# Two attention stages in a woven Trainium2 kernel: first attention by query only and turned by TensorE, second attention's scores copied and masked by a GpSimd select

## The chip, the cores and the metric

The program runs on one core of one Trainium2 chip (the chip has eight). The metric is device time in microseconds of one execution: 2770.05 us for the kernel before, the median of three runs (2768.12 to 2773.97). A core has five engines that work beside each other, each through its own instructions in order: TensorE (PE, with its weight loads shown apart as PEld), VectorE (DVE), ScalarE (ACT), GpSimd (POOL) and SyncE (SP), which here starts the DMAs. [...]

## The reference, cut to what matters

Two layers over x, 16 batches of 256 tokens by 256 channels, float32 throughout:

```python
x = x + _L0_attn_ref(_L0_cond_ref(x, f, f, ...), ...)      # cross attention, then the first attention
x = x + _L0_ffn_ref(_L0_cond2_ref(x, ...), ...)            # a category's matrix, then a quantized feed-forward
x = x + _L1_attn_ref(_L1_cond_ref(x, ...), ...)            # diffusion, then the second attention
x = x + _L1_ffn_ref(_L1_cond2_ref(x, ...), ...)            # an expert's projection, then a mixture of experts
```

The change touches the two causal attentions. The first has 16 heads of width 16 over the 256 tokens:

```python
scores = jnp.einsum('bhtd,bhsd->bhts', q, k) / jnp.sqrt(jnp.float32(Dh))
scores = jnp.where(causal, scores, -jnp.inf)
probs = jax.nn.softmax(scores, axis=-1)
out = jnp.einsum('bhts,bhsd->bhtd', probs, v)
```

The second has 16 heads of width 64 over segments of 128 tokens, with 16 learned keys and values ahead of each segment's own:

```python
mask = (j < p) | (j - p <= i)
scores = jnp.where(mask, scores, NEG_INF)
attn = jax.nn.softmax(scores, axis=-1)
out = jnp.einsum('bhij,bhjd->bhid', attn, v)
```

## The kernel before, in words

`program` runs `woven` (everything up to the second attention, for all batches) and then `mixture` (the last feed-forward, line 1266 and on). The change touches `woven` alone.

`woven` has a stage for each step of a batch, written as a Python generator that yields one instruction at a time: stage_a (cross attention and the first attention's projection), stage_m and stage_e (first attention), stage_gate, stage_up and stage_down (quantizing the feed-forward's weights, once), stage_y and stage_f (category matrix and feed-forward), stage_d (diffusion), stage_p and stage_u (second attention's projections of q, k and of v), stage_g (its scores), stage_v (its values and output), stage_c (an early start of the mixture) and stage_fill. `weave` (line 188) merges them while the program is built: it keeps a clock for each engine, takes at each step the instruction that could start first by the cost model in `Unit.cost` (line 167), ties by the stage's place in the list, and issues it. So the order of each engine's queue is fixed at build time, by planned durations. All instructions of the woven part carry line 163, where they are issued, and groups are told apart by the names of their tiles.

Stages wait for each other through counters in `g.done`: J counts batches projected, M and E halves through stage_m and stage_e, A batches whose first attention is done, D batches diffused, P, U, G and V the items of the second attention (four a batch, 64 in all). Stage_a projects batch b when `M >= 2 * b and A >= b - 1` (line 413). PSUM is handed out as two pairs (two banks each) and four singles; `quad` takes both pairs. Stage_fill keeps TensorE busy with matmuls of the identity (tile `ident` alone) in planned gaps until the first batch's first attention is done.

The first attention treats the heads of a batch in two halves of eight. The 128 channels of a half lie on the partitions: four groups of 32, two heads in each. `blocks` spreads a transposed q or k by head (b_diag) so that a group's matmul of 32 rows gives the scores of its two heads; the four groups' matmuls go to different rows of TensorE. A half passes twice through its scores:

- `heads_maximum` (stage_m): transposes q and k (b_qk to b_qkT), scores with the queries on the partitions, adds the mask and takes the maximum on VectorE, and exponentials on ScalarE, of which only the sums are kept. Maxima and reciprocal sums (tile `shift`) are transposed into `b_rows`.
- `heads_exponential` (stage_e): the scores again, now with the keys on the partitions (b_diag, b_qkT), and by matmuls of `ones` with b_sdiag the negated maxima on top in PSUM. One exponential for each pair (b_e), and a GpSimd select that zeroes the keys behind the query.
- `heads_values`: the values' matmuls on b_e (32 columns of weights), the reciprocal sums spread over the channels by a matmul (`spread`), two VectorE steps to b_u and a GpSimd sum to b_oT. Stage_e then applies the output projection (wout, b_oT).

The second attention's `scores4` (stage_g) makes the scores of four heads for two segments (keys, f_q), adds the mask on VectorE while copying from PSUM to f_prob, and then takes maxima (f_stat), exponentials and sums, and GpSimd's product with the reciprocal sums. `values4` (stage_v) transposes f_prob on TensorE (f_prob to f_pT), multiplies with the values (f_pT, f_v to f_oT) and applies the output projection (wo, f_oT). `project4` (stage_p) makes q and k: VectorE products, GpSimd sums (f_t), and eight DMAs for an item that move the rows into f_q and keys.

Of the kernel before, what the change touches and what calls it, by code (L numbers as in the profile page):

```python
# [19 lines left out]
P = 128  # L20
# [128 lines left out]
class Unit:  # L149
# [17 lines left out]
    def cost(self, fn, outs, ins):  # L167
        if self.name == "SP":
            return 0.5
        if self.name == "PE":  # L170
            if fn == "transpose":
                return 0.13
            lhsT, rhs = ins
            rows, cols, t = lhsT.shape[0], row_size(lhsT), row_size(rhs) / 555

            if rows <= 64:
                return SIDE
            return max(t / 3.5, 0.1) if cols <= 32 else max(t / 1.7, 0.14) if cols <= 64 else t
        fixed, each = COSTS[self.name]
        n = max(row_size(x) for x in outs[:1] + ins)  # L180
        if fn == "reciprocal":
            each = 0.006
        if fn == "affine_select":
            fixed, each = 0.2, 0.00095
        return fixed + each * n + (0.3 if len(outs) > 1 else 0)
# [108 lines left out]
S_BUFS = 2  # L294
# [19 lines left out]
def woven(k):  # L314
    nc, tc = k.nc, k.tc
    with ExitStack() as ctx:
        g = Stages()
        g.k, g.a, g.B, g.ident = k, k.a, k.B, k.ident
        g.pe, g.dve, g.act = Unit("PE", nc.tensor), Unit("DVE", nc.vector), Unit("ACT", nc.scalar)
        g.pool, g.sp = Unit("POOL", nc.gpsimd), Unit("SP", nc.sync)  # L320
        pool = lambda name, bufs, **kw: ctx.enter_context(tc.tile_pool(name=name, bufs=bufs, **kw))
        g.w = pool("w", 1)
        g.xp = pool("x", 5)
        g.f_, g.l_ = pool("sf", 1), pool("sl", 1)

        g.attention0 = tc.tile_pool(name="sa", bufs=1, side="right")
        g.a_ = g.attention0.__enter__()
        space = bass.MemoryType.PSUM
        psum = pool("psum", 1, space=space)
        g.pairs = [psum.tile([P, 2, 512], F32, name=f"pair{i}") for i in range(PAIRS)]  # L330
        g.singles = [psum.tile([P, 512], F32, name=f"single{i}") for i in range(8 - 2 * PAIRS)]
        g.zT = {}
        g.v1, g.live, g.kT, g.qk, g.v = {}, {}, {}, {}, {}
        g.taking = False
        g.x, g.io, g.done = {}, {}, {"J": 0, "U": 0, "Y": 0, "H": 0, "W": 0, "D": 0, "Z": 0, "A": 0, "M": 0, "E": 0, "F": 0, "P": 0, "G": 0, "V": 0, "L": 0, "R": 0, "C": 0}
        with tc.manual_schedule():
            weave([stage_a(g), stage_m(g), stage_e(g), stage_gate(g), stage_up(g), stage_down(g), stage_y(g), stage_f(g), stage_v(g), stage_g(g), stage_p(g), stage_u(g), stage_d(g), stage_c(g), stage_fill(g)])
# [80 lines left out]
def head_constants(g):  # L418
# [9 lines left out]
    g.halves, g.place = small("halves", 2), small("place", 32)  # L428
    yield g.dve.tensor_reduce(g.halves, g.ident.rearrange("p (g r d) -> p r g d", g=4, r=2), AX.XY, ALU.add)
    yield g.dve.tensor_reduce(g.place, g.ident.rearrange("p (g w) -> p w g", g=4), AX.X, ALU.add)  # L430
    g.ones, g.spread = small("ones", P), small("spread", P)
    yield g.pool.memset(g.ones, 1.0)
    own = g.ident.rearrange("p (g w) -> p g w", g=4)[:, :, 2:4]
    yield g.pool.tensor_copy(g.spread.rearrange("p (g r d) -> p g r d", g=4, r=2), own.unsqueeze(3).to_broadcast([P, 4, 2, DH0]))
    g.shift = small("shift", 2, P)
    yield g.pool.memset(g.shift, 0.0)


def stage_m(g):

    for i in range(2 * g.B):
        yield lambda: g.done["J"] > i // 2 and i < g.done["E"] + 2
        g.kT[i] = yield from heads_maximum(g, i)
# [3 lines left out]
def stage_e(g):  # L447

    for b in range(g.B):
        oT = g.a_.tile([P, 2, S], F32, name="b_oT", tag="b_oT")  # L450
        for c in range(2):
            yield lambda: g.done["M"] > 2 * b + c
            kept = g.kT.pop(2 * b + c)
            prob = yield from heads_exponential(g, *kept)
            yield from heads_values(g, b, c, prob, kept[1], oT)
# [166 lines left out]
def blocks(g, name, src, which, bufs):  # L622


    t = g.a_.tile([P, 2, S], F32, name=name, tag=name, bufs=bufs)
    wide = [P, 2, S]
    yield g.pool.tensor_tensor(t, src.unsqueeze(1).to_broadcast(wide), which.unsqueeze(2).to_broadcast(wide), ALU.mult)
    return t


def heads_maximum(g, i):
# [4 lines left out]
    t = g.a_.tile([P, 2, S], F32, name="b_qkT", tag="b_qkT", bufs=2)  # L636
# [8 lines left out]
    kd = yield from blocks(g, "b_diag", t[:, 1, :], g.halves, 2)  # L645
    shift = g.shift
    by_head = shift.rearrange("p s (g w) -> p s g w", w=32)
    sums = g.a_.tile([P, 2, 4, 2], F32, name="b_sums", tag="b_sums", bufs=2)
    for st in (1, 0):
# [6 lines left out]
        scores = []  # L656
        for two in four:
            sc = g.a_.tile([P, 2, 2, n], F32, name="b_s", tag="b_s", bufs=S_BUFS)
            raw = two[:, :, : 2 * n].rearrange("p i (r k) -> p i r k", r=2)
            mask = g.k.mask[:, 2 * P - n :].unsqueeze(1).unsqueeze(1).to_broadcast([P, 2, 2, n])  # L660
            yield g.dve.tensor_tensor(sc, raw, mask, ALU.add)
            g.pairs.append(two)
            scores.append(sc)
        for j0, sc in zip((0, 2), scores):
            yield g.dve.tensor_reduce(by_head[:, st, j0 : j0 + 2, 0:2], sc, AX.X, ALU.max, negate=True)
        for j0, sc in zip((0, 2), scores):
            for j in (j0, j0 + 1):
                for r in range(2):
                    x, one = sc[:, j - j0, r, :], lambda t, w: t[:, st, j, w : w + 1]
                    yield g.act.activation(x, x, AF.Exp, bias=one(by_head, r), accum_out=one(sums, r))  # L670
    yield g.dve.reciprocal(by_head[:, :, :, 2:4], sums)
    rows = g.a_.tile([P, S], F32, name="b_rows", tag="b_rows", bufs=2)
    one = yield from single(g, shift)
    pt = one[:, :S]
    for st in range(2):
        yield g.pe.transpose(pt[:, st * P : (st + 1) * P], shift[:, st, :], g.ident)
    yield copy_(g, rows, pt)
    g.singles.append(one)
    return t, rows


def heads_exponential(g, t, rows):


    qd = yield from blocks(g, "b_diag", t[:, 0, :], g.halves, 2)
    sd = yield from blocks(g, "b_sdiag", rows, g.place[:, 0:2], 1)
    prob = []
    for kb in range(2):
        n = (2 - kb) * P
        four = yield from quad(g, t, qd, sd)  # L690
        out = lambda j: four[j // 2][:, j % 2, : 2 * n]
        for j in range(4):
            lhsT, rhs = t[row32(j, 32), 1, kb * P : (kb + 1) * P], qd[row32(j, 32), :, kb * P :]
            yield g.pe.matmul(out(j), lhsT, rhs, start=True, stop=False)
        for j in range(4):
            yield g.pe.matmul(out(j), g.ones[row32(j, 32), :], sd[row32(j, 32), :, kb * P :], start=False, stop=True)
        for two in four:
            e = g.a_.tile([P, 4, n], F32, name=f"b_e{kb}", tag=f"b_e{kb}", bufs=2)
            yield g.act.activation(e.rearrange("p (i r) k -> p i (r k)", i=2), two[:, :, : 2 * n], AF.Exp)
            g.pairs.append(two)  # L700
            own = e[:, :, 0:P]
            yield g.pool.affine_select(
                out=own,
                in_=own,
                compare_op=ALU.is_ge,
                fill=0.0,
                base=0,
                pattern=[[0, 4], [1, P]],
                channel_multiplier=-1,
            )  # L710
            prob.append(e)
# [3 lines left out]
def heads_values(g, b, c, prob, rows, oT):  # L715


    v = g.v[b]
    po = yield from single(g, *prob, v)
    by_half = po.rearrange("p (r s) -> p r s", r=2)  # L720
    for kb in range(2):
        for j in range(4):
            lhsT = v[:, kb, c * P + 32 * j : c * P + 32 * (j + 1)]
            e = prob[2 * kb + j // 2][:, 2 * (j % 2) : 2 * (j % 2) + 2, :]
            yield g.pe.matmul(by_half[row32(j, 32), :, kb * P :], lhsT, e, start=kb == 0, stop=kb == 1)
    one = yield from single(g, rows)
    yield g.pe.matmul(one[:, :S], g.spread, rows, start=True, stop=True)
    rinv = rows
    yield copy_(g, rinv, one[:, :S])
    g.singles.append(one)  # L730
    u = g.a_.tile([P, 2, S], F32, name="b_u", tag="b_sdiag")
    for r in range(2):
        yield g.dve.scalar_tensor_tensor(u[:, r, :], by_half[:, r, :], g.halves[:, r : r + 1], rinv, ALU.mult, ALU.mult)
    g.singles.append(po)
    yield g.pool.tensor_tensor(twined(oT[:, c : c + 1, :]), untwined(u[:, 0:1, :]), untwined(u[:, 1:2, :]), ALU.add)
# [446 lines left out]
def scores4(g, n, q, keys):  # L1182
# [10 lines left out]
    mask = g.k.mask[:, P - PM :].unsqueeze(1).unsqueeze(1).to_broadcast([P, 2, 2, w])  # L1193
    by_head = lambda t: t.rearrange("p (a j) w -> p j a w", a=2)
    for st in range(2):
# [8 lines left out]
        yield g.dve.tensor_tensor(by_head(prob[:, st]), raw, mask, ALU.add)  # L1204
        g.pairs.append(two)
    for st in range(2):
# [547 lines left out]
```

## Time and profile before

| what | value |
|---|---|
| median of three runs | 2770.05 us (2768.12 to 2773.97) |
| profiled execution | 2773.39 us, span 2771.7 us |
| granted TensorE clock, mean | 0.978 of full speed |
| TensorE busy | 2594.5 us (94% of the span) |
| VectorE, ScalarE, GpSimd busy | 1430.1, 1083.4 and 980.5 us (52%, 39%, 35%) |
| first and last output projection of the first attention | start at 121.8 and about 1566 us |
| last matmul of the woven part | ends about 1809 us |

The span's busy shares mix two programs: the woven part, in which four engines share the work, and the mixture behind it, in which TensorE is busy for 952 of 961 us. Stretches and groups of the woven part alone tell more than the page's first line. In a line of a group stand: line, engine, operation, tile written and tiles read, shape (rows by columns of weights, then partitions by elements), count; then the busy time in us and the mean of one in ns; then the engine's idle time just before the group and what ended it. A float32 matmul shows as two records, a transpose as one.

### The profile page before, as it was taken

What the parts mean: (1) busy time and instruction counts of PE and PEld (TensorE: products, weight loads), DVE (VectorE), ACT (ScalarE), POOL (GpSimd) and SP (SyncE); (2) the same over time, 40 slices, a digit from 0 to 9 for tenths busy, and PEclk for the clock granted to TensorE, in tenths of its full rate; (3) what the DMA queues carried; (4) which work ended last, traced back from release to release, by engine and by line L of the source; (5) the groups of instructions that cost most, each with busy time, mean ns of one, the idle gap of its engine ahead of it and who ended that gap; (6) DMA issues with size and microseconds to landing.
All of it is one profiled execution on the core that took longest, in us unless ns stands there. A gap on an engine that the chain in (4) does not pass through costs nothing. (4 is left out here: it accounts for less than half of the span.)

```text
span 2771.7 us, 40010 instructions
## 1 busy us (share of the span) xinstructions
PE 2594.5 (94%) x13855; PEld 1893.2 (68%) x13855; DVE 1430.1 (52%) x2712; ACT 1083.4 (39%) x3304; POOL 980.5 (35%) x1121
## 2 busy tenths in 40 slices
PE   8879898998999999999999898899999999999999
PEld 6645576666766666676665676555566888888866
DVE  7466676776777776777777665333340000000023
ACT  2444435444545544644554433322222222222221
POOL 5344545444445445454555433223320000000035
PEclk9999999999999999999999999899999999999999
DMA  4121333233343333233332254141111455556523
GB/s 127 51 77 37 97 116 97 87 103 101 94 126 106 96 96 122 62 114 118 104 95 86 73 157 125 58 131 51 50 45 69 150 190 197 186 194 199 200 84 107
DMA packets 249661, 303.64 MB, mean 110 GB/s; under 512 B 43120, under 2 KB 216432, under 8 KB 240112
## 3 DMA queue, kind: packets, MB, share of 16 engines
q1 hardware_dynamic: 243312, 284.26, 32.8%
q0 software_dynamic: 6144, 16.79, 1.9%
q8 instruction: 112, 1.84, 0.3%
q14 instruction: 93, 0.76, 0.1%
HBM read 206.85 MB, written 60.56 MB: 96 GB/s over the span
## 5 line engine op out<-in xcount | busy, mean ns | idle before, releaser
L1398 POOL DMA_INDIRECT got<-osort,pos_o x64 | 62.3, 974 | 626.4 <-ACT hT L1331 586.0
L1380 ACT ACTIVATE ehT<-bank,own_b 128x256 f32<-128x256 f32 x280 | 132.5, 473 | 349.1 <-PE bank L49 349.1
L163 POOL TENSOR_TENSOR f_t<-f_t,f_t 128x256 f32<-128x256 f32 x256 | 187.5, 750 | 210.2 <-DVE f_t L163 189.2
L163 PE MATMUL single<-e_zT,wq 128*128 128x256 f32 x1024 | 250.8, 388 | 0.0
L49 PE MATMUL bank<-ysT,w 128*128 128x256 f32 x1120 | 247.6, 379 | 0.2 <-ACT ysT L105 0.2
L49 PE MATMUL bank<-w,ehT 128*128 128x256 f32 x1120 | 247.5, 379 | 0.0
L163 ACT ACTIVATE b_s<-b_s,shift 128x128 f32<-128x128 f32 (+1 forms) x512 | 225.3, 444 | 55.4 <-DVE shift L163 55.4
L49 PEld LDWEIGHTS bank<-ysT,w 128*128 128x128 f32 x1120 | 212.7, 190 | 29.3 <-ACT ysT L105 0.5
L163 ACT ACTIVATE f_prob<-f_prob,f_stat 128x144 f32<-128x144 f32 x512 | 205.5, 405 | 60.3 <-DVE f_stat L163 60.2
L49 PEld LDWEIGHTS bank<-w,ehT 128*128 128x128 f32 x1120 | 210.2, 190 | 27.2
L163 PEld LDWEIGHTS single<-e_zT,wq 128*128 128x128 f32 x1024 | 190.0, 193 | 38.7 <-issue 11.0
L163 ACT ACTIVATE b_e<-pair 128x512 f32<-128x512 f32 (+1 forms) x128 | 99.9, 804 | 118.6 <-PE pair L163 118.1
L163 PE MATMUL single<-wo,f_oT 128*128 128x256 f32 x512 | 134.4, 397 | 12.0 <-DVE f_oT L163 9.9
L163 PE MATMUL pair<-b_diag,b_qkT 32*128 32x512 f32 (+1 forms) x1024 | 133.4, 545 | 12.5 <-POOL b_diag L163 5.9
L1388 DVE TENSOR_TENSOR eo<-bank,eb 128x512 f32<-128x512 f32 x35 | 24.2, 691 | 234.4 <-PE bank L49 234.4
L163 DVE TENSOR_TENSOR x<-x,single 128x512 f32<-128x512 f32 (+1 forms) x112 | 68.1, 608 | 132.9 <-PE single L163 129.9
L163 DVE TENSOR_TENSOR b_s<-pair,mask 128x512 f32<-128x512 f32 (+1 forms) x128 | 116.3, 949 | 19.6 <-PE pair L163 19.1
L163 PE MATMUL single<-wv,e_zT 128*128 128x256 f32 x512 | 122.2, 382 | 1.6 <-DVE x L163 1.6
L163 POOL TENSOR_TENSOR f_prob<-f_prob,f_stat 128x1024 f32<-128x1024 f32 x64 | 123.1, 1924 | 0.0
L1347 DVE COPY own_b<-b1t 128x8 f32<-128x8 f32 x35 | 5.9, 174 | 222.3 <-ACT ehT L1380 222.3
L1493 POOL DMA_INDIRECT ysort<-r_y,r_posi x64 | 62.4, 975 | 164.0 <-DMA ysort<-r_y,r_posi 105.4
L163 PEld LDWEIGHTS single<-wo,f_oT 128*128 128x128 f32 x512 | 97.0, 196 | 32.7 <-DVE f_oT L163 10.9
(313 smaller groups left out, 5366.2 us busy)
## 6 DMA issues: line engine op xcount, KB each, us to landing
w<-in_w SPq DMA_DIRECT2D x70, 1024.0 KB, 5.3
wq<-in_w_qk SPq DMA_DIRECT2D x128, 256.0 KB, 3.2
ysort<-zero SPq DMA_DIRECT2D x32, 1024.0 KB, 6.6
wv<-in_w_v SPq DMA_DIRECT2D x64, 256.0 KB, 3.7
f_q<-f_t SPq DMA_DIRECT2D x256, 64.0 KB, 2.0
keys<-f_t SPq DMA_DIRECT2D x256, 64.0 KB, 2.0
wo<-in_w_out SPq DMA_DIRECT2D x64, 256.0 KB, 3.5
ys<-ysort SPq DMA_DIRECT2D x35, 256.0 KB, 2.7
```

The lines of the kernel that those rows point to most:

```text
L49: nc.tensor.matmul(out, lhsT, rhs, start=start and i == 0, stop=stop and i == last)
L163: return Op([(self.name, self.cost(fn, outs, aps), lambda: call(*args, **kw))], outs, aps)
L1347: nc.vector.tensor_copy(b1, r.b1t[:, t, :])
L1380: nc.scalar.activation(hT[:, f, :], ph, AF.Gelu_apprx_tanh, bias=b1[:, f : f + 1])
L1388: nc.vector.tensor_tensor(o, po, b2.unsqueeze(1).to_broadcast([P, 2, D]), ALU.add)
L1398: nc.gpsimd.indirect_dma_start(out=g, out_offset=None, in_=k.osort[:, :], in_offset=bass.IndirectOffsetOnAxis(ap=r.pos_o[:, i, t : t + 1], ...
L1493: nc.gpsimd.indirect_dma_start(out=k.ysort[:, :], out_offset=bass.IndirectOffsetOnAxis(ap=posi[:, i, t : t + 1], axis=0), in_=ys[t], in_of ...
```

## The change

The first attention passes through its scores once. `heads_maximum` and `heads_exponential` become `heads_softmax`: with the queries on the partitions, it masks only the blocks on the diagonal on VectorE, copies the left block of the second 128 queries by ScalarE or VectorE, takes the maxima, the exponentials with their sums in place, the reciprocals, and GpSimd's product. `heads_values` then transposes the probabilities on TensorE (b_e), 24 blocks of 128x128 a half, copies them to b_pT, and runs the same values' matmuls on these; the two heads of a group are put together by two scaled steps instead of the spread matmul, b_u and the GpSimd sum. The tiles ones, spread, place and shift go. Stage_m now waits until the first two of the four head groups of the half before have been turned (counter T).

The second attention's `scores4` copies the scores by ScalarE or VectorE (`copy_` leaves the choice to `weave`) and masks them by a GpSimd select on the 128 own keys. Three costs in the planner's model are changed (a transpose 0.13 to 0.115, columns per us 555 to 580, the factor for narrow weights 1.7 to 1.5), and stage_v moves behind stage_d in the list of stages.

```diff
             if fn == "transpose":
-                return 0.13
+                return 0.115
             lhsT, rhs = ins
-            rows, cols, t = lhsT.shape[0], row_size(lhsT), row_size(rhs) / 555
...
                 return SIDE
-            return max(t / 3.5, 0.1) if cols <= 32 else max(t / 1.7, 0.14) if cols <= 64 else t
+            return max(t / 3.5, 0.1) if cols <= 32 else max(t / 1.5, 0.14) if cols <= 64 else t
...
-            weave([stage_a(g), stage_m(g), stage_e(g), stage_gate(g), stage_up(g), stage_down(g), stage_y(g), stage_f(g), stage_v(g), stage_g(g), stage_p(g), stage_u(g), stage_d(g), stage_c(g), stage_fill(g)])
+            weave([stage_a(g), stage_m(g), stage_e(g), stage_gate(g), stage_up(g), stage_down(g), stage_y(g), stage_f(g), stage_g(g), stage_p(g), stage_u(g), stage_d(g), stage_v(g), stage_c(g), stage_fill(g)])
...
 def stage_m(g):
 
     for i in range(2 * g.B):
-        yield lambda: g.done["J"] > i // 2 and i < g.done["E"] + 2
-        g.kT[i] = yield from heads_maximum(g, i)
+        yield lambda: g.done["J"] > i // 2 and g.done["T"] >= 2 * i - 1
+        g.kT[i] = yield from heads_softmax(g, i)
         g.done["M"] = i + 1
 
 
@@ -450,9 +442,7 @@
         oT = g.a_.tile([P, 2, S], F32, name="b_oT", tag="b_oT")
         for c in range(2):
             yield lambda: g.done["M"] > 2 * b + c
-            kept = g.kT.pop(2 * b + c)
-            prob = yield from heads_exponential(g, *kept)
-            yield from heads_values(g, b, c, prob, kept[1], oT)
+            yield from heads_values(g, b, c, g.kT.pop(2 * b + c), oT)
             g.done["E"] += 1
...
+    kd = g.a_.tile([P, 2, S], F32, name="b_diag", tag="b_diag")
+    wide = [P, 2, S]
+    yield g.pool.tensor_tensor(
+        kd, t[:, 1, :].unsqueeze(1).to_broadcast(wide), g.halves.unsqueeze(2).to_broadcast(wide), ALU.mult
+    )
+    prob = {}
+    mask = g.k.mask[:, P:].unsqueeze(1).unsqueeze(1).to_broadcast([P, 2, 2, P])
     for st in (1, 0):
         n = (st + 1) * P
...
+        stat = g.a_.tile([P, 3, 8], F32, name="b_stat", tag="b_stat", bufs=4)
+        for jp, two in enumerate(four):
+            e = prob[st, jp] = g.a_.tile([P, 4, n], F32, name=f"b_e{st}", tag=f"b_e{st}", bufs=3)
+            raw = two[:, :, : 2 * n].rearrange("p j (r k) -> p j r k", r=2)
+            sc = e.rearrange("p (j r) k -> p j r k", r=2)
+            yield g.dve.tensor_tensor(sc[:, :, :, n - P :], raw[:, :, :, n - P :], mask, ALU.add)
+            if st:
+                yield copy_(g, sc[:, :, :, :P], raw[:, :, :, :P])
             g.pairs.append(two)
+        for jp in range(2):
+            e, own = prob[st, jp], slice(4 * jp, 4 * jp + 4)
+            yield g.dve.tensor_reduce(stat[:, 0, own], e, AX.X, ALU.max, negate=True)
+            for h in range(4):
+                one = lambda w: stat[:, w, 4 * jp + h : 4 * jp + h + 1]
+                yield g.act.activation(e[:, h, :], e[:, h, :], AF.Exp, bias=one(0), accum_out=one(1))
+            yield g.dve.reciprocal(stat[:, 2, own], stat[:, 1, own])
+            yield g.pool.tensor_tensor(e, e, stat[:, 2, own].unsqueeze(2).to_broadcast([P, 4, n]), ALU.mult)
     return prob
...
+def heads_values(g, b, c, prob, oT):
+
+
+    v, turned = g.v[b], []
+    for jp in range(2):
+        t = g.a_.tile([P, 4, 3, P], F32, name="b_pT", tag="b_pT", bufs=2)
+        e = prob[0, jp]
+        one = yield from single(g, e)
+        pt = one.rearrange("p (h q) -> p h q", h=4)
+        for h in range(4):
+            yield g.pe.transpose(pt[:, h, :], e[:, h, :], g.ident)
+        yield copy_(g, t[:, :, 0, :], pt)
+        g.singles.append(one)
+        e = prob[1, jp]
+        for h0 in (0, 2):
+            one = yield from single(g, e)
+            pt = one.rearrange("p (h k q) -> p h k q", h=2, k=2)
+            for h in range(2):
+                for kb in range(2):
+                    yield g.pe.transpose(pt[:, h, kb, :], e[:, h0 + h, kb * P : (kb + 1) * P], g.ident)
+            yield copy_(g, t[:, h0 : h0 + 2, 1:, :], pt)
+            g.singles.append(one)
+        g.done["T"] += 1
+        turned.append(t.rearrange("p h k q -> p h (k q)"))
+    po = yield from single(g, *turned, v)
...
+            pT = turned[j // 2][:, 2 * (j % 2) : 2 * (j % 2) + 2, :]
+            rhs = pT[:, :, S:] if kb else pT[:, :, :S]
+            yield g.pe.matmul(by_half[row32(j, 32), :, kb * P :], lhsT, rhs, start=kb == 0, stop=kb == 1)
+    which, own = lambda r: g.halves[:, r : r + 1], twined(oT[:, c : c + 1, :])
+    first, other = untwined(by_half[:, 0:1, :]), untwined(by_half[:, 1:2, :])
+    a = g.act.activation(own, first, AF.Copy, scale=which(0))
+    d = g.dve.tensor_scalar(own, first, which(0), None, ALU.mult)
+    yield Op(a.choices + d.choices, a.outs, a.ins)
+    yield g.dve.scalar_tensor_tensor(own, other, which(1), own, ALU.mult, ALU.add)
     g.singles.append(po)
...
-    mask = g.k.mask[:, P - PM :].unsqueeze(1).unsqueeze(1).to_broadcast([P, 2, 2, w])
...
-        yield g.dve.tensor_tensor(by_head(prob[:, st]), raw, mask, ALU.add)
+        yield copy_(g, by_head(prob[:, st]), raw)
         g.pairs.append(two)
+        own = prob[:, st, :, PM:]
+        yield g.pool.affine_select(
+            out=own, in_=own, compare_op=ALU.is_ge, fill=NEG, base=0, pattern=[[0, 4], [-1, P]], channel_multiplier=1
+        )
```

## The prediction

> **What bounds the kernel now.** I read the page first, then the busy time in stretches, then who waited for whom on TensorE, then the groups of TensorE by shape. The profiled execution took 2773.4 us (span 2771.7 us; the median of the runs is 2770.05 us, so 3.3 us lie between it and the figure I forecast). The woven part, which the change touches, ends near 1810 us.
>
> ```profile
> 122.00:1640.00 1518.00, 1389.21 (x8285) 973.07 (x8285) 1093.53 (x1850) 723.80 (x2492) 729.17 (x833) 0.97 0.32 96
> 1640.00:1782.00 142.00, 120.94 (x731) 96.18 (x731) 71.48 (x117) 48.82 (x193) 49.56 (x60) 0.90 0.44 133
> ```
>
> Columns: stretch, length, then busy time of PE, PEld, DVE, ACT, POOL, the granted clock, DMA. From 122 to 1640 us TensorE is busy for 92%, VectorE for 72%, ScalarE and GpSimd for 48% each. So TensorE's own work is the bound, plus 129 us in which it waits:
>
> ```profile
> PE single L163 <- POOL d_h L163: 35.2, 13, 8.4
> PE single L163 <- DVE shift L163: 16.7, 10, 4.8
> PE pair L163 <- ACT b_e L163: 10.0, 12, 1.2
> ...
> PE single L163 <- POOL f_prob L163: 6.9, 6, 1.7
> ```
>
> Totals in us, times, longest. The second and third lines belong to steps that the change removes; the first and last stay.
>
> ```profile
> L163 PE MATMUL single<-ident,f_prob 128*128 128x128 f32 x512 | 82.1, 293 | 25.0 <-POOL f_prob L163 25.0
> L163 PE MATMUL pair<-b_diag,b_qkT 32*128 32x512 f32 x512 | 79.5, 657 | 7.5 <-POOL b_diag L163 5.9 <-DVE b_v L163 0.8 <-ACT a_e L163 0.8
> L163 PE MATMUL single<-ident 128*128 128x128 f32 x468 | 62.1, 288 | 1.6 <-POOL ident masks.py:199 1.6
> L163 PE MATMUL pair<-b_diag,b_qkT 32*128 32x256 f32 x512 | 53.9, 434 | 5.0 <-DVE b_s L163 2.8 <-ACT b_e L163 2.2
> L163 PE MATMUL pair<-b_sdiag,ones 32*128 32x512 f32 x256 | 38.4, 639 | 1.1 <-POOL b_sdiag L163 0.8
> L163 PE MATMUL pair<-b_sdiag,ones 32*128 32x256 f32 x256 | 25.2, 394 | 0.0
> L163 PE MATMUL single<-b_rows,spread 128*128 128x256 f32 x64 | 22.4, 431 | 1.7 <-DVE d_th L163 1.7
> L163 PE MATMUL single<-ident,shift 128*128 128x128 f32 x64 | 14.2, 306 | 19.1 <-DVE shift L163 16.7 <-DVE f_stat L163 1.5 <-ACT d_hT L163 0.9
> ```
>
> A transpose is one record, any other matmul two. The mean (293 ns) is a record's latency; what it costs in a stream is the busy total divided by the count.
>
> **TensorE's work.** There are 32 halves (16 batches, 2 halves of the heads). Each loses the second scores by key (half of the two b_diag groups), the ones matmuls, spread and the shift transposes. By the busy totals that is (79.5 + 53.9)/2 + 38.4 + 25.2 + 22.4 + 14.2 = 167 us. By pitch, from a group's start to the next one's start less idle time, averaged over 122 to 1640 us of the timeline, a half loses 1.06 + 0.65 + 1.07 + 0.58 + 0.59 + 0.33 = 4.28 us, in all 137 us. Added are 24 transposes a half, 768 in all. By the busy total of f_prob's transposes (82.1/512 = 0.160 us) that is 123 us; by their pitch (four in 0.53 us) 102 us; by the tightest pitch seen, 0.44 us for four, 84 us. Net: -44 us by busy totals, -35 us by pitches. I take pitches, which leave the tail before a wait out. The value matmuls keep their shapes and count.
>
> The Trainium skill, "TensorE: Matmul & The Clock Gate", Part 4, puts a 128x128 transpose at about 275 ns in a kernel's context; this trace has that as latency (293 ns), and four start within 0.53 us. By the page's figure as a price, 768 would cost 211 us and the change would lose 74 us on TensorE.
>
> The built order of TensorE's instructions holds 272 filler matmuls ahead of the first output projection where there were 234, since the first batch's chain is longer than the other work at the start. 38 x 62.1/234 = +10 us; nothing hides that. TensorE's sum is -25 us.
>
> **The other engines, per kernel.** GpSimd loses 128 selects of 0.678 us, 32 b_diag of 1.105, 32 b_sdiag of 1.164 and 32 b_oT of 0.842 us, 186 us; it gets 64 products of 1024 elements (1.924 us, the row of f_prob's product), 64 of 512 (about 1.1, b_diag's row) and 128 selects on f_prob (0.678): 280 us. That is +94 us, from 48% to 54% of the long stretch. VectorE loses 128 masks on f_prob (0.750), 64 masks of 1024 (1.216), 64 b_u (0.479), 32 reciprocals, 26 b_rows, some 222 us. It gets 64 masks of 512 (0.68), 61 of the 64 left-block copies, 51 of the 192 b_pT copies and 29 of the 128 f_prob copies (0.68 to 0.75), 128 small reciprocals (about 0.17) and 36 b_oT steps: some 180 us. ScalarE loses 64 exponentials of 1.020 and 64 of 0.588 us and 38 b_rows (0.372), 117 us; it gets 141 b_pT copies (0.585), 99 f_prob copies (about 0.64) and 28 b_oT (0.488), 160 us. All of this lies beside TensorE; it costs only where TensorE's next instruction needs it.
>
> **Waits.** Gone: shift (16.7 us) and b_sdiag (0.8). The waits for pairs held by b_e (10.0) I halve: half as many quads are taken, but the copies hold them as the exponential did. New: 192 groups of transposes wait for GpSimd's product. The nearest row is f_prob, the same chain of exponential, reciprocal, product, transpose: 6.9 us in 128 groups, so 10 us. The far end is d_h, 35.2 us in 64 groups, so 106 us; the near end is nothing. I take 10. On GpSimd, in order, the selects and products are queued ahead of d_h and of f_t's rotary sums (which release the q and keys transfers): d_h's 35.2 us by the load, 54/48, gives +5. A select that waits for its copy holds up the same.
>
> In the tail (1640 us on) only the second attention is left, and its chain sets the pace: eight waits on f_prob make 18.1 us from there. Each score now goes through GpSimd twice more, 2 x 0.68 us, of which one runs beside the other tile's reduction: 9 items x 1 us = +9. A long wait also costs clock:
>
> ```profile
> 1748.97 1.97 PE L163 MATMUL single<-ident,f_prob 128*128 128x128 f32 x8 [3.22 <-POOL f_prob L163]
> 1750.87 2.29 PE L163 MATMUL single<-f_pT,f_v 128*64 128x128 f32 x16
> ```
>
> After 3.22 us of idling these take about double (1.09 us each elsewhere), after 1.64 us they do not. One more such cold start is 4 us. The same page, Part 1, halves the clock after an idle window of about 3.4 us; the trace agrees in kind, but has a cold start after 2.33 us already. By the rule alone, none of the longer waits but one would be cold.
>
> Waits: -16.7 - 0.8 - 5 + 10 + 5 + 9 + 4 = +5. **Sum:** -25 + 5 = -20 us, so 2753 against the profiled execution and 2750 us against the median. Bounds: cheap transposes and no new waits give -137 + 84 + 10 - 27 = -70 (2700); the dear end of the waits gives some +76 (2846), which I hold to be far off.
>
> **Rivals.** (1) A larger gain: the exponential and the reciprocal finish early, the new waits stay near zero, GpSimd's queue has room. For: 46% of it is idle. Against: it works in order. -70 to -35 us, at about 2715 us.
>
> (2) Nothing to be measured, within 0.2% (5.5 us, about what a measurement can tell): d_h and f_prob wait 20 us more than I count. About 2770 us.
>
> (3) Slower: the first attention's own loop becomes the bound. A batch's projection waits until both halves of the batch before have their scores finished, and a half starts only when the first pair of the half before has been turned. In the trace a half goes from b_qk's transposes to the next one's in 32.4 us (1012.15 to 1044.52) and the projection before it takes 14.6 (from 997.59), so the loop is 2 x 32.4 + 14.6 = 79 us of a period of (1567.8 - 121.8)/15 = 96.4 us. The change adds per half the first twelve transposes (1.6), GpSimd's last product (1.1) or all four (6.0), and up to two copies (1.4): 3 to 9 us alone. From 8 or 9 us the loop is as long as the period; queueing decides, since all engines are shared. At 11 us it is 101 us a period, 15 x 5 = +75, of which TensorE's lighter work takes back the 35: about 2810 us. For: the new stages are in series, GpSimd's product included, and the built order puts the next projection directly behind the last scores of a batch in places. Against: between the last scores and the first transposes of a half it puts some 10 us of other work.
>
> **Chances.** Forecast (2735 to 2764) 0.45, larger gain 0.17, no change 0.10, slower 0.28. So faster 0.62, same 0.10, slower 0.28. The range 2702 to 2802 leaves out most of the far end of (3) and a little of (1); the forecast's own is 2735 to 2764.
>
> **What would show it.** No shift, b_sdiag or spread groups; 768 transposes of b_e at about 0.16 us busy each; TensorE's busy time down by 25 to 45 us, VectorE's by some 40, GpSimd's up by some 90. The wait for POOL b_e near 10 us: above 50 says that (3) or the far end holds. The last output projection at 1545 to 1570 us from the start says whether the loop binds: later than 1600 is rival (3). A tail of 240 us or more behind it says that the select's latency costs more than counted. I am wrong if TensorE's busy share in the long stretch falls clearly under 0.92.

## The result, and the profile after

| | before | after |
|---|---|---|
| median of 20 runs each | 2772.69 us | 2777.08 us |
| ratio, with its 95% interval | | 1.0016 (1.0009 to 1.0023) |
| profiled execution, span | 2771.7 us | 2774.4 us |
| TensorE busy | 2594.5 us | 2566.9 us |
| VectorE, ScalarE, GpSimd busy | 1430, 1083, 980 us | 1437, 1119, 1088 us |
| first and last output projection of the first attention (start) | 121.8, 1567.8 us | 118.4, 1592.7 us |
| end of the woven part | 1809.5 us | 1812.6 us |
| TensorE idle up to that end | 167 us | 198 us |

The change makes the kernel 0.16% slower, inside the 0.2% that the prediction treats as no change. TensorE's busy time went down by 28 us, and the time it waits went up by 31 us. The stretch from the first to the last output projection of the first attention, before and after (columns: stretch, length, busy time of PE, PEld, DVE, ACT, POOL, granted clock, DMA):

```profile
121.80:1567.80 1446.00, 1322.83 (x7914) 921.54 (x7913) 1041.97 (x1765) 698.50 (x2409) 699.43 (x799) 0.97 0.32 96
118.40:1592.70 1474.30, 1325.73 (x7753) 973.59 (x7752) 1087.97 (x1897) 740.99 (x2538) 807.81 (x831) 0.96 0.31 95
```

TensorE's idle time in it (length less busy time) went from 123 to 149 us, which is 25 of the 31 us. Behind it the woven part got shorter, from 241.7 to 219.9 us.

The two stretches that the prediction used, in the profile after, with the same columns:

```profile
122.00:1640.00 1518.00, 1366.00 (x7983) 1004.54 (x7982) 1112.61 (x1938) 756.62 (x2582) 824.80 (x851) 0.96 0.32 97
1640.00:1782.00 142.00, 113.26 (x662) 87.97 (x662) 61.92 (x102) 55.43 (x194) 60.48 (x75) 0.92 0.41 123
```

In the long stretch TensorE is busy for 90% where it was 92%, GpSimd for 54% where it was 48%. Who waited for whom on TensorE in that stretch (totals in us, times, longest):

```profile
PE single L163 <- POOL d_h L163: 23.5, 11, 3.7
PE single L163 <- POOL f_prob L163: 18.6, 7, 6.7
PE single L163 <- DVE f_pT L163: 18.4, 10, 5.7
PE single L163 <- POOL c_y L163: 12.3, 7, 4.1
PE single L163 <- ACT f_oT L163: 8.4, 12, 1.9
```

The waits for shift are gone as forecast. Of the 10.0 us for pairs held by b_e the prediction kept half; 3.8 us are left (they now end with VectorE). The waits that grew are elsewhere. f_prob went from 6.9 to 18.6 us, and three more rows stood like this in the kernel before (c_y belongs to the category stage, which the change does not touch):

```profile
PE single L163 <- DVE f_pT L163: 4.4, 5, 1.7
PE single L163 <- POOL c_y L163: 2.4, 3, 1.3
PE single L163 <- ACT f_oT L163: 2.1, 6, 0.4
```

TensorE's new groups and its fillers (`ident` alone), after the change:

```profile
L163 PE MATMUL single<-ident,b_e 128*128 128x128 f32 x768 | 115.9, 282 | 3.6 <-POOL b_e L163 1.3 <-DVE f_t L163 1.0 <-ACT b_pT L163 1.0
L163 PE MATMUL single<-ident,f_prob 128*128 128x128 f32 x512 | 77.9, 286 | 33.7 <-POOL f_prob L163 33.1 <-DVE f_t L163 0.5
L163 PE MATMUL single<-ident 128*128 128x128 f32 x544 | 67.6, 283 | 1.6 <-POOL ident masks.py:199 1.6
```

768 transposes of the probabilities cost 115.9 us and wait 3.6 us in all: the first attention's new steps are cheap and rarely late. f_prob's transposes wait 33.7 us where they waited 25.0.

### The profile page after: what moved, and what is told of

It reads as the page before. It is cut to its first block, busy times and chain, and to the rows that moved or that the text cites. A ratio compares the mean times of both kernels' runs of the same rounds, so it can differ in the third digit from the quotient of the medians.

```text
span 2774.4 us, 39526 instructions
## 1 busy us (share of the span) xinstructions
PE 2566.9 (93%) x13547; PEld 1926.0 (69%) x13547; DVE 1437.2 (52%) x2791; ACT 1118.5 (40%) x3384; POOL 1088.2 (39%) x1150
## 5 line engine op out<-in xcount | busy, mean ns | idle before, releaser
L163 ACT ACTIVATE b_e<-b_e,b_stat 128x128 f32<-128x128 f32 (+1 forms) x512 | 226.4, 444 | 131.3 <-DVE b_stat L163 128.1
L163 POOL TENSOR_TENSOR f_t<-f_t,f_t 128x256 f32<-128x256 f32 x256 | 200.6, 799 | 195.0 <-DVE f_t L163 136.4
L163 POOL TENSOR_TENSOR b_e<-b_e,b_stat 128x512 f32<-128x512 f32 (+1 forms) x128 | 191.0, 1492 | 134.5 <-DVE b_stat L163 110.6
L163 ACT COPY b_pT<-single 128x512 f32<-128x512 f32 x141 | 80.4, 589 | 139.5 <-PE single L163 139.4
L163 POOL TENSOR_SCALAR_AFFINE_SELECT f_prob<-f_prob 128x512 f32<-128x512 f32 x128 | 93.3, 729 | 81.7 <-ACT f_prob L163 68.4
```

What stands on the lines that cost most here:

```text
L163: return Op([(self.name, self.cost(fn, outs, aps), lambda: call(*args, **kw))], outs, aps)
```

## The experiments

Three theories were open: the second attention's selects give the gain back (A), the planner's new values make a worse order (B), the new first attention has waits of its own (C). All medians below are of 4 to 10 runs beside runs of the kernel before on the same chip (2770.8 to 2774.0 us there); the ratios are to those.

**The parts one by one.** `first_only` takes the second attention back, `second_only` puts it into the kernel before:

```diff
-        yield copy_(g, by_head(prob[:, st]), raw)
+        yield g.dve.tensor_tensor(by_head(prob[:, st]), raw, mask, ALU.add)
         g.pairs.append(two)
-        own = prob[:, st, :, PM:]
-        yield g.pool.affine_select(
...
```

> The changed kernel with the second attention as before (mask added by VectorE, no GpSimd select); first attention, planner's costs and list of stages as changed. Theory A (the selects on GpSimd give back what the first attention's part gains): about 2750 us, 0.992 of before, and TensorE's waits on POOL f_prob and DVE f_pT near the 25 and 5 us of before. Theory B (the planner's new costs and list of stages make a worse order): about as the changed kernel, 1.000 to 1.003. Theory C (the new first attention brings waits of its own that eat its gain): 1.000 to 1.003 as well, with TensorE's waits in the woven part near 195 us.

> The kernel before with only the second attention's change (copy by ScalarE or VectorE, GpSimd select). Theory A: slower by about 20 us, 1.006 to 1.009. Theories B and C: 0.998 to 1.002.

`planner_only` puts the new costs and list into the kernel before, `after_old_planner` the old ones into the changed kernel:

```diff
-                return 0.13
+                return 0.115
...
-            rows, cols, t = lhsT.shape[0], row_size(lhsT), row_size(rhs) / 555
+            rows, cols, t = lhsT.shape[0], row_size(lhsT), row_size(rhs) / 580
...
```

and likewise the factor for narrow weights and the place of stage_v in the list.

> The kernel before with only the three planner costs and the place of stage_v changed; every instruction is the same, only the order differs. Theory B: slower by 10 to 25 us, 1.004 to 1.009. Theories A and C: 0.998 to 1.002.

> The changed kernel with the three planner costs and the list of stages of before. Theory B: faster than before by 15 to 25 us, 0.991 to 0.995. Theories A and C: 0.999 to 1.004.

The remaining two of the eight combinations, built from the same edits:

> The first attention's change alone, planned with the costs and the list of stages of before. If the first attention's change gains whatever the plan: 2735 to 2755 us, 0.986 to 0.993 (its lighter TensorE work, 25 to 45 us). If the 43 us of the first run need the new planner values: 0.996 to 1.005.

> The kernel before with the second attention's change and the new planner values. If the second attention's change costs 28 to 46 us whatever the plan, and the new values cost the old first attention 41 us: 2842 to 2860 us, 1.025 to 1.031. If the second attention's price is mostly the scatter of the plans: anywhere between 1.005 and 1.02.

Measured, as medians in us and ratios with their intervals:

| attentions | old planner values | new planner values |
|---|---|---|
| as before | 2772.7 | planner_only 2814.4, 1.0155 (1.0140 to 1.0169) |
| first changed | first_old_planner 2788.4, 1.0060 (1.0046 to 1.0074) | first_only 2730.6, 0.9849 (0.9835 to 0.9862) |
| second changed | second_only 2801.9, 1.0105 (1.0090 to 1.0121) | second_new_planner 2788.6, 1.0065 (1.0049 to 1.0080) |
| both | after_old_planner 2799.8, 1.0100 (1.0083 to 1.0116) | after 2777.1, 1.0016 (1.0009 to 1.0023) |

No part has a price of its own. The first attention's change alone costs 16 us with the old values and gains 84 us with the new (2730.6 against 2814.4). The second attention's change costs 29 us on the kernel before and 11 us on top of the first, both with the old values; with the new ones it costs 46 us on top of the first and gains 26 us in `second_new_planner`. The new values cost 42 us in the kernel before and gain 58 us under the first attention's change.

A, B and C each fit some cells and fail in others. `planner_only` is slower, as B said, but by more than B's range; `after_old_planner` is slower than the changed kernel, where B had it faster. `second_only` is a little slower than A's range, and `first_only` is faster than A's 0.992, but TensorE's waits in it (10 us on f_prob and 28 us on VectorE's f_pT in its woven part) are not the 25 and 5 us that A expected. `first_old_planner` came out just above its second range, `second_new_planner` within its second. What differs from cell to cell besides the parts is the whole order of instructions, which is drawn again for each.

**The selects in an unchanged order.** To price a part without drawing a new order, the planner was left to plan the changed kernel as it is, and only what is issued was altered:

```diff
-        yield g.pool.affine_select(
+        op = g.pool.affine_select(
...
+        op.choices = [(e, t, lambda: None) for e, t, _ in op.choices]
+        yield op
```

> The changed kernel in its own plan, instruction for instruction, but the 128 selects of the second attention are not issued, so that its scores are not masked. If GpSimd's selects are what gives back the gain (time in the chain and in its queue): 2735 to 2755 us, 0.986 to 0.993, with the waits on POOL f_prob and DVE f_pT in the woven part down from 36 and 20 us to 25 and 5 or less. If the plan around them is (places fixed for a longer chain): 0.997 to 1.002.

> The changed kernel in its own plan, but at the place of each copy of the second attention's scores VectorE adds the mask, as before the change, and no select is issued; all other instructions stay in their order. If the selects cost and VectorE has room: as the kernel without selects, 0.986 to 0.994. If VectorE's 99 more steps of 0.75 us (74 us on an engine busy for 73% of the long stretch) cost as much as the selects: 0.998 to 1.006.

Without the selects: 2756.7 us, 0.9945 (0.9932 to 0.9959), so 20 us less than the changed kernel. That lies between what the two readings expected, nearer to the first, though the waits on f_prob and f_pT stayed (33 and 20 us up to the end of the woven part, where 36 and 20 stood); half of the gain is idle time of TensorE, spread over many small waits, and half is busy time, for the same matmuls:

```profile
117.60:1572.00 1454.40, 1316.02 (x7753) 966.32 (x7753) 1080.86 (x1898) 741.77 (x2538) 729.40 (x725) 0.97 0.32 97
```

This is the stretch between the first and the last output projection, 1474.3 us long in the changed kernel. All of the 20 us lie in it; behind it both kernels take 220 us to the end of the woven part. With VectorE's mask in the place of copy and select: 2783.5 us, 1.0042 (1.0028 to 1.0057), 6 us more than the changed kernel, as the second reading had it. So in this order the selects cost 20 us, and doing the same masking on VectorE costs slightly more.

**Other draws of the order.** Two numbers of the planner that have nothing to do with the change were moved, which leaves every kind of work as it is and only orders it anew. Two things aside: the fillers go from 210 to 241 matmuls in the kernel before and from 253 to 273 in the changed one (each about 0.27 us busy), and copies move between ScalarE and VectorE, where `weave` is free to choose.

```diff
-HOP = 0.15
+HOP = 0.16
...
-TURN = 0.02
+TURN = 0.03
```

one of the two at a time; the fee `TURN` also at 0.04. `after_old_order` keeps the new costs and puts stage_v back in the list.

> The kernel before with one number of the planner moved that has nothing to do with the change: the small fee for switching between stages on TensorE, 0.02 to 0.03. Same instructions, another order. If an order drawn by the planner is worth little by itself: 0.998 to 1.002. If the scatter of orders is what the sums of the last runs show (before stands 15 to 41 us below its own variants): 1.005 to 1.016.

> The changed kernel with the same fee moved from 0.02 to 0.03. Little scatter: 0.999 to 1.004. Scatter of 1%: anywhere from 0.99 to 1.012.

> The first attention's change alone, planned with the new values, and the same fee moved from 0.02 to 0.03. If its 43 us are the first attention's: 0.983 to 0.988. If they are a lucky order: 0.99 to 1.006, the value with the old planner.

> The changed kernel with the new costs but stage_v at its old place in the list. If the list's place matters by itself: near the 1.010 of the old planner; if the costs do: near 1.002; if orders scatter: either, or something else.

> The kernel before, the planner's hop between engines 0.15 to 0.16 us; same instructions in another order. If the order before was a good draw among its own: slower, 1.003 to 1.016. If not: 0.99 to 1.00.

> The changed kernel, hop 0.15 to 0.16 us. If the change gains by its lighter TensorE work and its own first order was a poor draw: 0.965 to 0.995. If the 2677 us were the one lucky draw: 0.998 to 1.01.

> The kernel before, switching fee 0.04. By scatter around its other draws: 1.003 to 1.016. If a larger fee makes plans better for both kernels: under 0.99.

> The changed kernel, switching fee 0.04. If a larger fee makes better orders for it: 0.96 to 0.975. If it is scatter: 0.975 to 1.01.

| planner | kernel before | changed kernel |
|---|---|---|
| each with its own values | 2772.7 | 2777.1, 1.0016 |
| each with the other's values | 2814.4, 1.0155 | 2799.8, 1.0100 |
| own values, fee 0.03 | 2792.0, 1.0069 (1.0047 to 1.0092) | 2676.9, 0.9657 (0.9637 to 0.9677) |
| own values, hop 0.16 | 2777.8, 1.0027 (1.0015 to 1.0038) | 2743.9, 0.9900 (0.9882 to 0.9918) |
| own values, fee 0.04 | 2770.6, 0.9996 (0.9986 to 1.0006) | 2762.6, 0.9963 (0.9951 to 0.9976) |

`after_old_order` took 2769.7 us, 0.9987 (0.9976 to 0.9997), and `first_turn` 2729.3 us, 0.9835 (0.9818 to 0.9853), like `first_only`. `after_old_order` is near neither the 1.010 nor the 1.002 of its two readings, and `after_turn` is faster than both of its expectations allowed (0.99 at the least). `before_turn4` was expected slower than the kernel before and is level with it, and `before_hop` is a little under its range; `after_turn4` falls in the range for scatter. Of three orders of the first attention's change alone, two gain 43 and 45 us on the kernel before and one loses 15.

The same changed kernel ran from 2676.9 to 2799.8 us, the kernel before from 2770.6 to 2814.4 us. Row by row of the table, the changed kernel stands at +4, -15, -115, -34 and -8 us to the one before, -33 us on average. The pairs are chosen, though: with the same planner values in both kernels, the first two differences are +27 us (old values) and -37 us (new). As two groups of five orders the kernels differ by -33 us with a standard error of some 22 us, and by -15 us if the one order at 2676.9 us is left out. So a gain on average is not shown, and the +4 us that the prediction was about lies well inside the scatter.

What the quicker order (`after_turn`) has is seen in the stretch between the first and the last output projection of the first attention, first in the changed kernel, then in `after_turn`:

```profile
118.40:1592.70 1474.30, 1325.73 (x7753) 973.59 (x7752) 1087.97 (x1897) 740.99 (x2538) 807.81 (x831) 0.96 0.31 95
```

```profile
116.60:1497.50 1380.90, 1292.99 (x7743) 954.68 (x7742) 1089.50 (x1906) 737.59 (x2521) 820.42 (x831) 0.99 0.33 102
```

The counts of instructions agree within a per cent on each engine, and so does the busy time of VectorE and ScalarE; GpSimd's is not lower either. TensorE waits 88 us instead of 149, and needs 33 us less for the same work, at a granted clock of 0.99 instead of 0.96. By the timeline, the changed kernel has 25 waits over 2 us in this stretch (78 us of them), the quicker order 8 (21 us), and the kernel before 10 (40 us). The quicker order's longest sums, in the same stretch:

```profile
PE single L163 <- POOL c_y L163: 16.8, 13, 4.1
PE single L163 <- POOL d_h L163: 12.3, 9, 2.7
PE single L163 <- DVE c_xT L163: 6.5, 9, 2.2
PE pair L163 <- POOL b_diag L163: 6.1, 6, 1.3
PE single L163 <- POOL f_prob L163: 5.1, 6, 1.8
```

f_prob (18.6 us in the changed kernel) and d_h (23.5 us) have fallen, f_pT has left the top, and c_y has grown (12.3 us). No single wait does it.

**The selects in the quicker order.** The same edit as above, under the fee of 0.03:

> The changed kernel in the order of the fee 0.03, instruction for instruction, without the 128 selects, so that the second attention's scores are not masked. If the selects cost what they did in the first order (20 us): 2650 to 2662 us, 0.956 to 0.960. If their price belonged to the poor order: 2668 to 2678 us, 0.963 to 0.966.

2665.0 us, 0.9611 (0.9595 to 0.9627): 12 us less than `after_turn`, between the two expectations. The selects cost something in both of these orders, and more in the one that waits more.

## Why the prediction was wrong, point by point

- **The step that failed is the sum of the waits, +5 us; it is +31 us** (198 against 167 us of idle time up to the woven part's end). The terms for the long stretch (-16.7 - 0.8 - 5 + 10 + 5) come to -7.5 us; between the first and the last output projection TensorE's idle time went up by 25 us. The terms for the tail (+9 + 4) come to +13 us; behind the last output projection it went up by 4.5 us. The sum carried the rows of the other waits over from the profile of before, as if they belonged to their stages. They belong to an order: f_pT on VectorE went from 4 to 20 us, c_y from 2 to 12, f_oT on ScalarE from 3 to 10 (on VectorE from 10 to 6), d_h from 35 down to 24. Of these the prediction named only d_h, and with the wrong sign. The other draws show that the order alone spreads the two kernels over 44 and 123 us; only the work that the change removes and adds on TensorE (137 and 102 us) stands in the sum with terms of that size.
- **The selects** were mis-sized and misplaced. The prediction counted +9 us for them in the tail, and a part of the +5 us on d_h. In the kept order they cost 20 us, all of it before the last output projection and none behind it. f_prob's waits grew by 11 us in all, near the 9 counted, but in the long stretch (6.9 to 18.6 us) and not from 1640 to 1782 us (18.1 to 17.5 us).
- **TensorE's work** came out at the number, -25 us forecast with the fillers and -28 us measured in the profiled execution, and the 768 transposes cost 115.9 us between the two prices of 102 and 123 us. That the number is so near is in part luck. By the traces' record of the clock, TensorE was busy for 106 us of the woven part at half clock before and for 123 us after. If work at half clock takes twice as long (the last section has matmuls that do), some 8 us of the busy time after are lost clock, and the change itself took off some 36 us (an estimate). In the quicker order TensorE's busy time is 2530.8 us, 64 us under the kernel before; by the same estimate 24 of these are clock regained.
- **The fillers** were wrong in effect: there are 38 more, but the first output projection starts 3 us earlier. The +10 us, counted as a stretch of their own, are not seen; the fillers' busy time rose by 5.5 us.
- **The removed waits** went as forecast (shift, b_sdiag, about half of b_e's). The wait of the new transposes for GpSimd's product was priced at 10 us and is 1.3 us; the far end of 106 us was far off indeed.
- **The range** of 2702 to 2802 us held the time, but the chances did not fit its width: 0.62 was given to a gain, with no term for the draw of the order. The five orders of each kernel (-33 us, standard error some 22) do not contradict the -20 us as a statement on many draws, nor do they show it. For one order the sum could not tell the sign: a draw decided it.
- **Rival 2** (d_h and f_prob wait 20 us more) gave the measured time with half the mechanism: the additional waiting is there, but mostly on other tiles.
- **Rival 3** (the first attention's loop as the bound) is not what happened: its last output projection came at 1592.7 us, a period of (1592.7 - 118.4)/15 = 98.3 us, but the same stages in the same series run at (1497.5 - 116.6)/15 = 92.1 us in the quicker order, and TensorE hardly waits for b_e.
- **VectorE** was to lose 40 us and gained 7; see the last section.
- **The signs.** One of the prediction's own signs of being wrong came: TensorE's busy share in the long stretch is 0.90, under 0.92. The last output projection at 1592.7 us lies between its two limits. The sign for the tail, 240 us or more, could not tell anything, since the kernel before has 241.7 us already.

What stays open: which property of an order makes it good. A larger fee is not it (0.03 gives 2676.9 us, 0.04 gives 2762.6), nor the place of stage_v. Whether the change gains on average over orders is not settled by five orders of each. The best kernel of the study is the changed one with the fee of 0.03, 2676.9 us, 3.4% under the kernel before.

## What to carry to other kernels

Where a planner draws the whole order of instructions at build time, a change of the work and a new draw come together; one measurement cannot tell them apart. Move an unrelated planner number by a little on both sides to learn the scatter first, and price a part by leaving it out of an order that is kept, not by planning again. A kernel whose order is among the best of its own draws will look better beside its successor's first draw than the change deserves (here the kernel before took 2772.7 us, and its other orders 2770.6 to 2814.4 us). Draw again before judging either, since the draw here was worth more than the change.

## What the runs showed of the hardware

Some of VectorE's steps that read and write SBUF took longer when they started while GpSimd was running an instruction; its copies from PSUM (the tiles `single` and `pair`, into which the matmuls write) did not, and neither did its reductions. The groups in the kernel before, then in the changed one (count, then busy us and mean ns):

```profile
L163 DVE SCALAR_TENSOR_TENSOR q_xn<-q_big,q_xn 128x704 f32<-128x704 f32 x64 | 67.8, 1059 | 4.1
L163 DVE TENSOR_SCALAR q_big<-q_big 128x704 int32<-128x704 int32 x32 | 22.7, 710 | 10.9 <-ACT q_big L163 10.9
L163 DVE TENSOR_SCALAR c_yT<-c_yT 128x512 int32<-128x512 int32 x16 | 8.3, 521 | 1.9 <-ACT c_yT L163 1.9
L163 DVE COPY f_pT<-single 128x512 f32<-128x512 f32 x38 | 25.9, 682 | 32.2 <-PE single L163 32.2
```

```profile
L163 DVE SCALAR_TENSOR_TENSOR q_xn<-q_big,q_xn 128x704 f32<-128x704 f32 x64 | 74.2, 1160 | 2.8 <-DVE q_big L163 0.5
L163 DVE TENSOR_SCALAR q_big<-q_big 128x704 int32<-128x704 int32 x32 | 29.6, 924 | 13.6 <-ACT q_big L163 13.6
L163 DVE TENSOR_SCALAR c_yT<-c_yT 128x512 int32<-128x512 int32 x16 | 19.9, 1242 | 4.9 <-ACT c_yT L163 4.9
L163 DVE COPY f_pT<-single 128x512 f32<-128x512 f32 x57 | 38.5, 681 | 27.0 <-PE single L163 26.6
```

c_yT goes from 521 to 1242 ns and the copy from PSUM stays at 681. The trace can be sorted by whether a GpSimd instruction was running when the step started. In the changed kernel 11 of the 16 c_yT steps started so and took 1619 ns on average, the other 5 took 413 ns; for q_xn it is 38 steps of 1348 ns and 26 of 886 ns. In the kernel before, 4 c_yT steps took 835 ns and 12 took 416 ns. The copies to f_pT took 681 ns beside GpSimd and 680 ns without, the reductions of f_prob to f_stat 741 and 740 ns. So the means rise because more of these steps start beside GpSimd, and because those that do take longer. Leaving out the selects alone, in the kept order, does not undo it (c_yT still takes 1081 ns).

The three groups add 25 us and account for about half of the 47 us by which VectorE missed its forecast. Smaller groups of the same kind (e_u, a_e) add some 14 us, and copies that the planner moved from ScalarE to VectorE some 12 us (f_pT, 38 to 57 of them, above all). GpSimd's own sums for the rotary step (f_t) went from 750 to 799 ns. The Trainium skill, "SBUF — State Buffer", section "SBUF: two separate sides", has VectorE and GpSimd share a pair of SBUF ports under a lock that is held for a whole instruction, against VectorE's faster modes and its steps with two SBUF inputs. The sorted times agree with that; that the lock is the reason is not shown by a run here.

A wait on TensorE costs more than its length. The changed kernel's order and the quicker one do the same work in the stretch shown; beside 61 us of idle time, 33 us of busy time separate them, along with the granted clock (0.96 and 0.99). By the traces' record of the clock, the changed kernel has 106 us of this stretch at half clock, in 23 pieces, with TensorE busy for 92.5 us of them; the quicker order has 34 us in 8 pieces, 32.5 us of them busy. The matmuls of the projections of q and k (e_zT with wq) start 216 ns apart at full clock and 427 ns apart at half clock (medians in the changed kernel). So the estimate for the busy time lost to the clock is (92.5 - 32.5)/2 = 30 us, nearly all of the 33. The Trainium skill, "TensorE: Matmul & The Clock Gate", Part 1, describes a clock that falls after idling and returns after some microseconds of work; the rows agree in kind. About a third of the difference between the two orders (33 of 93 us) lies in that busy time.
